# Attention rows: whole-array products issued as column tiles, and one transpose for two inputs

## The chip, the cores and the metric

The kernel runs on one core of one Trainium2 chip. The metric is device time in microseconds (us); lower is better. Before the change the median of three runs is 2716.82 us (2712.19 to 2721.92).

## What is computed

The input x has 256 rows of 256 positions with 128 channels. Layer 0 is an attention along each row, with a normalised x as query source and kv_x as key and value source; layer 1 is a spectral network on the result. The change touches layer 0 alone, which is, cut to what matters:

```python
def _L0_conv_ref(q_x, kv_x, bias1, bias2, wq, wk, wv, wg, bg, wo, bo):
    H = 4
    C_HIDDEN = 32
    q = split_heads(jnp.einsum('...qi,oi->...qo', q_x, wq)) / np.sqrt(C_HIDDEN)
    k = split_heads(jnp.einsum('...ki,oi->...ko', kv_x, wk))
    v = split_heads(jnp.einsum('...ki,oi->...ko', kv_x, wv))
    a = jnp.einsum('bshqd,bshkd->bshqk', q, k)
    a = a + bias1 + bias2
    a = jax.nn.softmax(a, axis=-1)
    o = jnp.einsum('bshqk,bshkd->bshqd', a, v)
    g = jax.nn.sigmoid(jnp.einsum('...qi,oi->...qo', q_x, wg) + bg)
    o = o * g
    return jnp.einsum('...qi,oi->...qo', o, wo) + bo

x = x + _L0_conv_ref(_gn(x), ...)
```

Everything is in 32-bit floats.

## The kernel before

`layer0` first reads x once for the statistics of the normalisation and folds them into wq and wg. Then the class `Rows` does the attention: its method `run` has a loop over i, the row, and rows are handled in pairs, g = i // 2. One pair of rows of x, and one of kv, is 512 positions by 128 channels. Layer 1 follows and isn't touched.

The order of instructions on each engine is the order of the program (`tc.manual_schedule` over PE, ACT, DVE, POOL and SP), so each queue can be read off the loop. The loop is a software pipeline: at row i it does the scores of row i, the projections of row i + 1, and the weighted sum of row i - 1. The parts are:

- `load` (L259) fetches a pair in pieces of 32 channels, two pairs ahead. `turn` (L283) brings it to channels on partitions with two DVE transposes of 32x32 blocks (L288), into buffers xT (four of them) and kvT (two).
- `project` (L292) makes q (L295) and k (L296) of a row: two products of the whole 128x128 array with 256 columns each. ACT copies them out (L300).
- `values` (L302) makes v of a pair with four products of 128 columns (L306) and the gate's input g with one of 512 (L312).
- `scores` (L319): eight products (L327), one for each head and half of the keys. A head has 32 channels, so each uses 32 rows of the array (shape 32*128), and four heads run side by side. ACT takes the exponential (L336).
- `weigh` (L345): DVE (L348) and POOL (L353) multiply by the exponential of bias1, POOL adds the two halves of the keys (L358).
- `attend` (L361): eight products with 32 output channels each (L368, shape 128*32, four side by side), and four with ones for the denominators (L373). DVE multiplies by the gate and divides (L379, L380, L381).
- `out` (L383): the output projection, one product of 512 columns (L386), the addition of x (L388), a transpose back (L390), and the store to x1d. `squares` (L401) and `spectrum` (L406) prepare layer 1: the latter reads the pair back and makes four products of 129 columns (L411).

PE's queue in an even row is L327, L295, L296, L386, L411, L368, L373; in an odd row L327, L295, L296, L306, L312, L368, L373. DVE's is L348, then L388 and L390 (even) or the two of L288 (odd), then L379, L380, L381. In PSUM, `ps_a` has four buffers, which the projections, v, g, wo, u and the weighted sum take in turn.

A PE shape is written as rows*columns of the array that an instruction uses: 128*128 is the whole array, 128*32 a column tile, 32*128 a row tile.

Of the kernel before, what the change touches and what calls it, by code (L numbers as in the profile page):

```python
# [10 lines left out]
FP = mybir.dt.float32  # L11
# [7 lines left out]
P = 128  # L19
# [177 lines left out]
class Rows:  # L197
# [72 lines left out]
    def run(self):  # L270
        tc, NS = self.tc, self.NS
        nc = tc.nc
        ctx, wT, rows, raw = self.ctx, self.wT, self.rows, self.raw
        b1T, b2T, bad = self.b1T, self.b2T, self.bad
        wk = ctx.enter_context(tc.tile_pool(name="l0wk", bufs=2))
        ps_s = ctx.enter_context(tc.tile_pool(name="l0s", bufs=1, space=PSUM))
        ps_a = ctx.enter_context(tc.tile_pool(name="l0a", bufs=4, space=PSUM))
        pairs = {}

        def row(s):  # L280
            return pairs[s // 2], slice(256 * (s % 2), 256 * (s % 2) + 256)

        def turn(g):  # L283
            t = raw.pop(g)
            p = pairs[g] = {}
            for k, (n, bufs) in enumerate((("xT", 4), ("kvT", 2))):
                p[n] = wk.tile([P, 512], FP, tag=n, name=f"{n}_{g}", bufs=bufs)
                nc.vector.transpose(p[n], t[:, k].rearrange("p b c -> p (b c)"))  # L288
            if g + 2 < NS // 2:
                self.load(g + 2)  # L290

        def project(s):  # L292
            p, q = row(s)
            ps = ps_a.tile([P, 512], FP, tag="a", name=f"qk_{s}")
            nc.tensor.matmul(ps[:, 0:256], self.wn["wq"], p["xT"][:, q], start=True, stop=True)  # L295
            nc.tensor.matmul(ps[:, 256:512], wT["wk"], p["kvT"][:, q], start=True, stop=True)  # L296
            r = rows[s] = {}
            r["qkT"] = wk.tile([P, 512], FP, tag="qkT", name=f"qkT_{s}")

            nc.scalar.activation(r["qkT"], ps, AF.Identity, bias=self.qb)  # L300

        def values(g):  # L302
            p = pairs[g]
            ps = ps_a.tile([P, 512], FP, tag="a", name=f"v_{g}")
            for c in range(4):
                nc.tensor.matmul(  # L306
                    ps[:, c * P : (c + 1) * P], p["kvT"][:, c * P : (c + 1) * P], wT["wv"], start=True, stop=True
                )
            p["v"] = wk.tile([P, 4, P], FP, tag="v", name=f"v_{g}")
            nc.scalar.copy(p["v"].rearrange("p c d -> p (c d)"), ps)  # L310
            p["g"] = ps_a.tile([P, 512], FP, tag="a", name=f"g_{g}")
            nc.tensor.matmul(p["g"], self.wn["wg"], p["xT"], start=True, stop=True)  # L312

        def gates(g):
            p = pairs[g]
# [67 lines left out]
        def out(g):  # L383
            p = pairs[g]
            ps = ps_a.tile([P, 512], FP, tag="a", name=f"wo_{g}")
            nc.tensor.matmul(ps, wT["wo"], p.pop("gate"), start=True, stop=True)  # L386
            xT = p["xT"]
            nc.vector.scalar_tensor_tensor(xT, ps, self.bo, xT, ALU.add, ALU.add)  # L388
            t = wk.tile([P, 16, 32], FP, tag="xb", name=f"x1b_{g}", bufs=1)
            nc.vector.transpose(t.rearrange("p b c -> p (b c)"), xT)  # L390
            pieces = self.x1d[2 * g : 2 * g + 2].rearrange("s (b t) c -> t (s b) c", t=32)
            for a in range(4):
                ch = slice(32 * a, 32 * a + 32)
                nc.sync.dma_start(pieces[:, :, ch], t[ch])
# [11 lines left out]
        def spectrum(g):  # L406
            x1 = pairs.pop(g)["x1"]
            ps = ps_a.tile([P, 512], FP, tag="a", name=f"u_{g}")
            for i in range(2):
                for j in range(2):  # L410
                    nc.tensor.matmul(  # L411
                        ps[:, 129 * i : 129 * i + 129], x1[:, i, j, :], self.adft[:, j, :],
                        start=(j == 0), stop=(j == 1),
                    )
            nc.scalar.copy(
                self.U[:, :, 2 * g : 2 * g + 2], ps[:, 0:258].rearrange("p (s f) -> p f s", s=2)
            )
# [3 lines left out]

        with tc.manual_schedule(engines={ENG.PE, ENG.Activation, ENG.DVE, ENG.Pool, ENG.SP}):
            turn(0)
            for i in range(-1, NS + 5):
                g, odd = i // 2, i % 2
# [7 lines left out]
                if i + 1 < NS:  # L433
                    project(i + 1)
# [5 lines left out]
                if odd and whole(g + 1):  # L440
                    values(g + 1)
                if odd and whole(g + 2):
                    turn(g + 2)
                if not odd and whole(g - 2):
                    out(g - 2)
                if not odd and whole(g - 3):
                    spectrum(g - 3)
                if 8 <= i < 16:
                    k, h = divmod(i - 8, 4)
# [131 lines left out]
def layer1(tc, I, C, ident, x1d, upool, U, Q2, groups, out):  # L581
# [9 lines left out]
    with ExitStack() as ctx:  # L591
# [908 lines left out]
        def first_modes(a, wp, mk, psum, gts):  # L1500
# [41 lines left out]
            for c in range(4):  # L1542
                synth_modes(wp, psum.pool, Z, P, h.Gd1, f"g1{a}", turned=True, chunk=c, ptag=psum.tag, gts=gts,
                            queues=(nc.gpsimd, nc.scalar))
                yield 2.4
                if c == 0:
                    yield next(tail)
                    yield next(tail)
                if c == 1:
                    run(tail)  # L1550
                    nc.vector.tensor_mul(h.bl0, h.bl0, h.row[:, 0:P])

                    ps = h.row
                    nc.tensor.matmul(ps[:, 256:257], blk[0], sig, start=True, stop=False)
                    nc.tensor.matmul(ps[:, 256:257], ident, ch[:, 2:3], start=False, stop=True)
                    nc.vector.tensor_copy(h.col[:, 13:14], ps[:, 256:257])
                    turned = mk("m", [P, 4, P], f"turned_{a}")
                    for j in range(4):
                        t = turned[:, j].rearrange("k (b d x) -> k b d x", b=2, d=2)
                        nc.vector.tensor_copy(  # L1560
                            t[:, :: (-1 if j & 2 else 1), :: (-1 if j & 1 else 1)],
                            ident.rearrange("k (b d x) -> k b d x", b=2, d=2),
                        )
                    for j in range(4):
                        nc.tensor.matmul(
                            ps[:, 260 + 2 * j : 262 + 2 * j], turned[:, j], h.col[:, 12:14],
                            start=True, stop=True,
                        )
                    nc.vector.tensor_copy(h.turn, ps[:, 260:268])
# [100 lines left out]
        def second_modes(a, wp, mk, psum, gts, yts):  # L1670
# [62 lines left out]
            for c in range(4):  # L1733
                if c == 2:
                    ps = psum.tile(f"cvps_{a}")
                    for i in range(4):
                        for r in range(2):
                            nc.tensor.matmul(
                                ps[:, 0:P], F[:, i, r, :], Z[:, i, r, :],
                                start=(i == 0 and r == 0), stop=(i == 3 and r == 1),  # L1740
                            )
                    cv = mk("m", [P, P], f"cv_{a}")
                    nc.vector.tensor_mul(cv, blk[1], ps[:, 0:P])
                synth_modes(wp, psum.pool, Z, P, h.Gd2, f"g2{a}", chunk=c, ptag=psum.tag, gts=gts,
                            queues=(nc.sync if a else nc.gpsimd, nc.scalar))
                yield 2.4
                if c == 0:
                    yield next(tail)
                    yield next(tail)
                if c == 1:  # L1750
                    run(tail)

                    for i in range(4):
                        r = slice(32 * i, 32 * i + 32)
                        v = h.row[r, 0:P].rearrange("k (b d x) -> k b d x", b=2, d=2)
                        nc.vector.tensor_tensor(
                            h.bl0[r].rearrange("k (b d x) -> k b d x", b=2, d=2),
                            v[:, :: (-1 if i & 2 else 1), :: (-1 if i & 1 else 1)],
                            bc(bc(blk[1][r, r], 1, 2), 1, 2), ALU.mult,
                        )  # L1760
# [362 lines left out]
```

## Time and profile before

| what | value |
|---|---|
| runs, median (lowest to highest) | 2716.82 us (2712.19 to 2721.92) |
| the profiled execution, and its span | 2722.32 us, 2720.5 us |
| instructions in the profile | 66879, of them 26560 products and 26560 weight loads on PE |
| PE busy | 2480.5 us (91%) |
| DVE busy | 2051.3 us (75%) |
| ACT busy | 1420.7 us (52%) |
| POOL busy | 1480.1 us (54%) |
| mean granted PE clock | 0.943 |
| row loop (first to last scores) | 114.6 to 1475.0 us |

The profile is one execution. PE is the matrix engine, PEld its weight loads, DVE, ACT and POOL the vector, scalar and general engines, SP the queue that issues transfers. The page cuts the span into 40 slices and gives a busy share in tenths for each. In a timeline line the columns are start, length, engine, source line, operation, output and inputs, and, for products, the shape and the elements of one instruction; xN says how many instructions are merged. In a line of a stretch the columns after the bounds are its length, then busy time and instruction count of PE, PEld, DVE, ACT and POOL, then granted clock, share of the transfer engines and GB/s. [...] consecutive products overlap and rates are read from start to start. One fp32 product of the source appears as two instructions.

### The profile page before, as it was taken

To read this page: it belongs to the slowest core of one execution; us is meant where nothing else is said; L and a number is where in the kernel's file an instruction comes from. 1 tells how busy PE (TensorE), PEld (TensorE's weight loads), DVE (VectorE), ACT (ScalarE), POOL (GpSimd) and SP (SyncE) were. 2 spreads that over 40 slices of the span, in tenths; PEclk is the share of its full clock that TensorE was granted. 3 is DMA by queue.
4 is the path that set the end of the run, shared out by engine and by line. 5 is a ranking of instruction groups with operands and counts; after the bars stand their busy time and mean duration, and the time that the engine had idled before them with its cause. 6 is when DMAs were issued, how large, how long until landed. Compare 5 with 4: busy or idle time off the path is not lost. (4 is left out here: it accounts for less than half of the span.)

```text
span 2720.5 us, 66879 instructions
## 1 busy us (share of the span) xinstructions
PE 2480.5 (91%) x26560; PEld 1648.3 (61%) x26560; DVE 2051.3 (75%) x3014; ACT 1420.7 (52%) x2718; POOL 1480.1 (54%) x1042
## 2 busy tenths in 40 slices
PE   7799999999999999999998899999988978898754
PEld 6566666666666666666665557787664566454522
DVE  7799999999999999999997438466645645455455
ACT  0277777778777787777776213100015501555232
POOL 0288999999998999999997003001135511111211
PEclk8899999999999999999999899999988987999755
DMA  9655555555555555555553010788987774997599
GB/s 369 192 98 98 101 99 101 101 100 99 102 100 100 100 98 101 100 98 103 99 101 71 20 57 1 250 273 266 316 290 237 258 240 129 333 358 258 185 378 345
DMA packets 1017841, 457.62 MB, mean 168 GB/s; under 512 B 831095, under 2 KB 947274, under 8 KB 1011129
## 3 DMA queue, kind: packets, MB, share of 16 engines
q1 hardware_dynamic: 977720, 363.13, 53.3%
q0 software_dynamic: 22912, 81.80, 7.8%
q10 hardware_dynamic: 16896, 8.39, 1.1%
q8 instruction: 212, 3.47, 0.5%
q14 instruction: 101, 0.82, 0.1%
HBM read 317.89 MB, written 135.27 MB: 167 GB/s over the span
## 5 line engine op out<-in xcount | busy, mean ns | idle before, releaser
L353 POOL TENSOR_TENSOR e<-e,b1T 128x1024 f32<-128x1024 f32 x256 | 606.1, 2367 | 203.8 <-ACT e L336 128.1
L358 POOL TENSOR_TENSOR es<-e 128x512 f32<-128x512 f32 x512 | 640.2, 1272 | 0.0
L380 DVE RECIPROCAL av<-av 128x256 f32<-128x256 f32 x256 | 452.1, 1766 | 8.8
L336 ACT ACTIVATE sc<-sc,b2T 128x512 f32<-128x512 f32 x512 | 338.8, 662 | 179.6 <-PE sc L327 171.3
L336 ACT ACTIVATE e<-sc,b2T 128x512 f32<-128x512 f32 x512 | 324.3, 692 | 0.0
L348 DVE TENSOR_TENSOR e<-sc,b1T 128x1024 f32<-128x1024 f32 x256 | 310.4, 1213 | 9.2 <-ACT sc L336 6.2
L327 PE MATMUL sc<-qkT 32*128 32x256 f32 x4096 | 293.6, 400 | 1.8 <-DVE e L348 1.8
L1381 PE MATMUL yps<-xt,mpT 128*128 128x256 f32 x1024 | 252.4, 398 | 27.1 <-DMA xt<-x1d 12.7
L368 PE MATMUL av<-e,v 128*32 128x256 f32 x4096 | 274.5, 385 | 2.2 <-DVE gate L381 1.9
L327 PEld LDWEIGHTS sc<-qkT 32*128 32x128 f32 x4096 | 185.3, 184 | 113.7 <-issue 100.9
L1381 PEld LDWEIGHTS yps<-xt,mpT 128*128 128x128 f32 x1024 | 195.8, 197 | 73.0 <-DVE yt L1393 17.0
L368 PEld LDWEIGHTS av<-e,v 128*32 128x32 f32 x4096 | 107.6, 109 | 159.3 <-PE v L306 94.0
L1397 POOL DMA_DIRECT2D yd<-yt x32 | 17.4, 545 | 320.7 <-DVE yt L1393 320.7
L295 PE MATMUL qk<-xT,wn_wq 128*128 128x256 f32 x512 | 179.4, 432 | 0.5 <-DVE hbg L230 0.5
L411 PEld LDWEIGHTS u<-adft,x 128*128 128x128 f32 x1024 | 135.7, 194 | 72.3 <-issue 62.9
L300 ACT ACTIVATE qkT<-qk,qb 128x512 f32<-128x512 f32 x256 | 174.0, 680 | 5.3 <-issue 5.3
L404 ACT ACTIVATE xT<-xT 128x256 f32<-128x256 f32 x256 | 104.4, 408 | 108.2 <-DVE x1b L390 106.3
L373 PE MATMUL av<-es,ones 128*32 128x256 f32 x2048 | 159.4, 379 | 1.4 <-POOL es L358 1.4
L1784 ACT ACTIVATE blocks<-h2ps,col 128x512 f32<-128x512 f32 x128 | 88.8, 778 | 128.5 <-PE h2ps L1248 128.5
L296 PE MATMUL qk<-kvT,wT_wk 128*128 128x256 f32 x512 | 152.7, 380 | 0.0
L379 DVE SCALAR_TENSOR_TENSOR gate<-gate,av 128x256 f32<-128x256 f32 x256 | 107.5, 420 | 53.5 <-PE av L373 40.1
L411 PE MATMUL u<-adft,x 128*128 128x129 f32 x1024 | 137.7, 278 | 8.5 <-DMA x<-x1d 8.4
(537 smaller groups left out, 4377.6 us busy)
## 6 DMA issues: line engine op xcount, KB each, us to landing
xt<-x1d SPq DMA_DIRECT2D x128, 512.0 KB, 6.7
xb<-in_x_dram SPq DMA_DIRECT2D x32, 1024.0 KB, 8.2
xk<-in_x_dram SPq DMA_DIRECT2D x512, 64.0 KB, 2.6
xk<-in_L_conv_kv_x_dram SPq DMA_DIRECT2D x512, 64.0 KB, 2.5
x1d<-x1b SPq DMA_DIRECT2D x512, 64.0 KB, 2.0
x<-x1d SPq DMA_DIRECT2D x128, 256.0 KB, 3.1
y<-yd SPq DMA_DIRECT2D x62, 512.0 KB, 7.0
gs<-Gd SPq DMA_DIRECT2D x384, 64.0 KB, 5.6
```

The lines of the kernel that those rows point to most:

```text
L295: nc.tensor.matmul(ps[:, 0:256], self.wn["wq"], p["xT"][:, q], start=True, stop=True)
L300: nc.scalar.activation(r["qkT"], ps, AF.Identity, bias=self.qb)
L327: nc.tensor.matmul(sc[h // 2][:, h % 2, c * 256 : (c + 1) * 256], qkT[p, 256 + c * P : 256 + (c + 1) * P], qkT[p, 0:256], start=True, stop ...
L336: nc.scalar.activation(r["e"][1][:, :, c, :] if hp else z, z, AF.Exp, bias=b2T[:, c, s : s + 1])
L348: nc.vector.tensor_tensor(r["e"][0].rearrange("p h c q -> p (h c q)"), r.pop("sc").rearrange("p h x -> p (h x)"), b1T[:, 0:2].rearrange("p ...
L353: nc.gpsimd.tensor_tensor(e1, e1, b1T[:, 2:4].rearrange("p h c q -> p (h c q)"), ALU.mult)
L358: nc.gpsimd.tensor_tensor(es, e[:, :, 0, :], e[:, :, 1, :], ALU.add)
L368: nc.tensor.matmul(ps[hd, 0:256], p["v"][:, 2 * (s % 2) + c, hd], r["e"][h // 2][:, h % 2, c, :], start=(c == 0), stop=(c == 1),)
L373: nc.tensor.matmul(ps[32 * h : 32 * h + 32, 256:512], self.ones, r["es"][h // 2][:, h % 2, :], start=True, stop=True,)
L380: nc.vector.reciprocal(rd, rd)
L411: nc.tensor.matmul(ps[:, 129 * i : 129 * i + 129], x1[:, i, j, :], self.adft[:, j, :], start=(j == 0), stop=(j == 1),)
L1381: nc.tensor.matmul(rows_of(ps[j]), mpT[:, sc, tt], by_turn(xt[:, sc])[:, j], start=(sc == 0), stop=False,)
```

## The change

All products of the row loop that used the whole array (q, k, v, g, wo, u) are issued as four products of 32 output channels or positions each, by the new helper `by_columns`: the same moving operand, a quarter of the stationary one, and the output to its quarter of the partitions. The two transposes of `turn` become one instruction, which writes x's and kv's part to two slots of a single buffer `turned` with six slots: four that rotate for x, two for kv. The rest of the loop, the order included, stays.

```diff
+        turned = wk.tile([P, 6, 512], FP, name="turned", bufs=1)
+
+        def by_columns(out, w, src, start=True, stop=True):
+            for h in range(4):
+                hd = slice(32 * h, 32 * h + 32)
+                nc.tensor.matmul(out[hd], w[:, hd], src, start=start, stop=stop)
...
         def turn(g):
             t = raw.pop(g)
-            p = pairs[g] = {}
-            for k, (n, bufs) in enumerate((("xT", 4), ("kvT", 2))):
-                p[n] = wk.tile([P, 512], FP, tag=n, name=f"{n}_{g}", bufs=bufs)
-                nc.vector.transpose(p[n], t[:, k].rearrange("p b c -> p (b c)"))
+            a, b = g % 4, 4 + g % 2
+            nc.vector.transpose(
+                turned[:, a : b + 1 : b - a].rearrange("p k (b c) -> p k b c", c=32), t
+            )
+            pairs[g] = {"xT": turned[:, a], "kvT": turned[:, b]}
...
-            nc.tensor.matmul(ps[:, 0:256], self.wn["wq"], p["xT"][:, q], start=True, stop=True)
-            nc.tensor.matmul(ps[:, 256:512], wT["wk"], p["kvT"][:, q], start=True, stop=True)
+            by_columns(ps[:, 0:256], self.wn["wq"], p["xT"][:, q])
+            by_columns(ps[:, 256:512], wT["wk"], p["kvT"][:, q])
...
             for c in range(4):
-                nc.tensor.matmul(
-                    ps[:, c * P : (c + 1) * P], p["kvT"][:, c * P : (c + 1) * P], wT["wv"], start=True, stop=True
-                )
+                by_columns(ps[:, c * P : (c + 1) * P], p["kvT"][:, c * P : (c + 1) * P], wT["wv"])
...
-            nc.tensor.matmul(p["g"], self.wn["wg"], p["xT"], start=True, stop=True)
+            by_columns(p["g"], self.wn["wg"], p["xT"])
...
-            nc.tensor.matmul(ps, wT["wo"], p.pop("gate"), start=True, stop=True)
+            by_columns(ps, wT["wo"], p.pop("gate"))
...
-                    nc.tensor.matmul(
-                        ps[:, 129 * i : 129 * i + 129], x1[:, i, j, :], self.adft[:, j, :],
-                        start=(j == 0), stop=(j == 1),
+                    by_columns(
+                        ps[:, 129 * i : 129 * i + 129], x1[:, i, j, :], self.adft[:, j, :], j == 0, j == 1
                     )
```

## The prediction

> **What bounds the kernel now.** I read the page's engine totals and its 40 slices first, to find the stage that the change touches and which engine fills it.
>
> ```profile
> PE   7799999999999999999998899999988978898754
> DVE  7799999999999999999997438466645645455455
> PEclk8899999999999999999999899999988987999755
> ```
>
> The row loop lies in slices 3 to 22 (its first product starts at 109 us, its last near 1498). PE and DVE both show nines there, at full clock. To tell which of the two is the limit, I asked for the busy time in a stretch of ten pairs of rows.
>
> ```profile
> 700.00:806.40 106.40, 106.40 (x1085) 68.60 (x1081) 100.62 (x121) 84.22 (x171) 96.48 (x60) 1.00 0.57 100
> ```
>
> PE is busy for all of the 106.40 us, DVE for 100.62, ACT 84.22, POOL 96.48. So a pair of rows takes 10.64 us, PE sets it, and DVE would need 10.06. The timeline of DVE agrees: in both rows it reaches L379 and has to wait for PE's L373.
>
> ```profile
> 709.25 1.21 DVE L348 TENSOR_TENSOR e<-sc,b1T 128x1024 f32<-128x1024 f32 x1
> 710.38 0.70 DVE L288 STREAM_TRANSPOSE xT<-xk 128x512 f32<-128x512 f32 x1
> 711.01 0.67 DVE L288 STREAM_TRANSPOSE kvT<-xk 128x512 f32<-128x512 f32 x1
> 711.97 0.42 DVE L379 SCALAR_TENSOR_TENSOR gate<-gate,av 128x256 f32<-128x256 f32 x1 [0.30 <-PE av L373]
> ```
>
> "Busy" on PE isn't work at its peak, so I took PE's own timeline of one pair and subtracted start from start.
>
> ```profile
> 704.07 1.06 PE L411 MATMUL u<-adft,x 128*128 128x129 f32 x8
> 705.06 1.07 PE L368 MATMUL av<-e,v 128*32 128x256 f32 x16
> 705.94 0.61 PE L373 MATMUL av<-es,ones 128*32 128x256 f32 x8
> 706.49 1.15 PE L327 MATMUL sc<-qkT 32*128 32x256 f32 x16
> 707.57 0.70 PE L295 MATMUL qk<-xT,wn_wq 128*128 128x256 f32 x2
> 708.10 0.59 PE L296 MATMUL qk<-kvT,wT_wk 128*128 128x256 f32 x2
> 708.53 1.05 PE L306 MATMUL v<-wT_wv,kvT 128*128 128x128 f32 x8
> 709.42 1.02 PE L312 MATMUL g<-xT,wn_wg 128*128 128x512 f32 x2
> 710.38 0.85 PE L368 MATMUL av<-e,v 128*32 128x256 f32 x12
> ```
>
> Each product in the source is two instructions here (two passes). L296 to L306 is 708.53 - 708.10 = 0.43 us with nothing in between: two passes of 256 columns, 0.215 each. That is the streaming rate, 0.43 us for each 256 columns of a whole-array product. L368 to L373 is 0.88 us for 16 instructions, which are four passes of four column tiles side by side: 0.22 a pass. So four 128x32 tiles together go as fast as one 128x128 product; tiling neither gains nor loses streaming time. What exceeds streaming sits at the changes of shape (128*128, 128*32, 32*128 in the rows):
> - 128*32 to 32*128 (L373 to L327): 0.55 - 0.43 = 0.12 before the first product, and L327's first weights 0.10 (1.08 from L327 to L295 = 0.86 streaming + 0.10 + 0.11 of the next change). 0.22 together.
> - 32*128 to 128*128: that 0.11, and L295's first weights, 0.53 - 0.43 = 0.10. 0.21 together.
> - 128*128 to 128*32: L312 to L368 is 0.96 for 0.86 of streaming, 0.10, and L368's first weights 0.88 - 0.86 = 0.02. 0.12 together.
>
> A row pays 0.22 + 0.21 + 0.12 = 0.55 us, a pair 1.10. Check: a pair streams 5636 columns (scores 1024, L368 and L373 1536, q and k 1024, v, g and wo 512 each, u 516) at 0.43/256, which is 9.47; 9.47 + 1.10 = 10.57 of 10.64.
>
> [...] 0.10 to 0.12 us at each change of shape, and none from L368 to L373, which changes tiles only. [...] The trace shows 0.10 exposed for L327 and L295 and 0.02 for L368. [...] in the trace 512 elements take 711.01 - 710.38 = 0.63 from start to start.
>
> **The change part by part.**
> *PE shapes.* q, k, v, g, wo and u become 128*32. Order and count of columns stay. Per row one change goes altogether (128*128 to 128*32, 0.12 us). [...] its first weights are 32 columns: 0.13 in place of 0.21, 0.08 saved. The change into L327 stays at 0.22. Saved: 0.20 us a row, 256 rows: 51 us. All of it is on PE, which is the bound, so it comes out of the time as long as PE remains the bound.
> *More PE instructions.* Per pair, q and k 8 instructions become 32, v 8 to 32, u 8 to 32, g and wo 2 to 8 each: 84 products more and as many weight loads. 216 PE instructions in 10.64 us become 384, or 38 per us. Tightest in v and u: 4 products and 4 loads for each 128 columns. Layer 1 of the same trace has exactly v's form (128*32, 128 columns), and a denser one:
>
> ```profile
> 2200.79 1.95 PE L1695 MATMUL f1ps<-YT,k_efwd 128*32 128x128 f32 x64
> ```
>
> ```profile
> 2313.81:2315.81 2.00, 2.00 (x132) 1.83 (x140) 0.06 (x1) 0.17 (x1) 1.49 (x2) 1.00 0.53 151
> ```
>
> 64 products are 16 passes; 1.95 less the tail of one product (0.27) is 1.68 over 15 passes plus the first load, 0.11 a pass, which is streaming rate. The second line has 132 products and 140 loads in 2 us, 136 instructions per us. So issue costs nothing in bursts. That 38 per us hold over 1.3 ms is less certain: layer 1 has 32 per us over 40 us (646 and 646 in 2300 to 2340). I take 0.
> *Four tiles on one moving operand.* L368, L373 and L1695 give each tile its own; here all four stream the same addresses. L644 (g11gp, 32*64) has two tiles on one moving operand and is the row of 136 per us, so at least two don't disturb each other. I take 0. Bounds: [...] a stretch f of the 3076 columns affected (5.17 us a pair) costs 661 us times f.
> *The merged transpose.* Two of 0.63 and 0.62 start to start become one of 1024 elements. The nearest row of that size is L348: 710.38 - 709.25 = 1.13. I take 1.15, 0.10 saved a pair. It is worth nothing: with PE at 10.64 - 0.40 = 10.24, DVE at 10.06 - 0.10 still waits. Both sides: free up to about 1.25 + 0.18 = 1.43 us; above that each 0.1 costs 13 us, and at 1.25 + 0.58 = 1.83 the gain is gone. Its wait covers the x and the kv pieces at once; both were loaded two pairs earlier and land in 2.6 us.
> *One buffer for all pairs.* Slots repeat after four (x) and two (kv) pairs as the separate buffers did. The instruction order on DVE shows the transpose waiting for its loads alone, and the products for what they waited for before. Cost 0.
> *What is late next.* A row falls to 5.12 us. POOL's 9.65 a pair (4.82 a row) fits. Waits into PE have room: L327 at 706.49 needs ACT's exp (L336, ended near 705.5) and L348 (705.1), 1.0 us; L368 at 705.06 needs DVE's previous L381 (704.0), 1.0 us; L373 needs POOL's sums of the row before (705.1), 0.8 us. Each loop of dependence turns with the same row time, so 0.2 us less leaves them short of binding. Next is DVE, 0.3 us a pair away.
>
> **The sum.** Profiled execution 2722.3 us (span 2720.5): less 51, 2671. The median of the three runs, 2716.8, is 5.5 lower, and I forecast from it: 2716.8 - 51 = 2666, rounded to 2667 for the first and last rows, which lack some of the changes.
>
> **Rivals.**
> 1. Half the gain. The entry from 32*128 into 128*32 occurs nowhere in the row loop before; if it costs 0.21 like the entry into 128*128, only 0.12 a row goes: 31 us, 2686. DVE or POOL binding in some rows would look the same. For it: that one transition is unseen, and DVE is close. Against: both its parts are seen singly.
> 2. No change: the stalls belong to waits on other instructions and not to the shapes, or DVE takes over because the merged transpose comes near 1.8 us. 2717. Against: the stall has one size at every change of shape, and from L368 to L373, which also waits on another engine, there is none.
> 3. Slower: the four tiles that stream one operand get in each other's way, in the six products that now do so. It decides from f = 51/661 = 7.7% on. At 15%, so that a pass of 256 columns takes 0.25 instead of 0.215, it costs 99 less 51: 2765. For it: no row shows four tiles on one operand, and the instruction stream nearly doubles for 1.3 ms. Against: L1695, L368 and L644 at the full rate.
>
> **How the numbers follow.** Forecast 0.65, half gain 0.17, no change 0.05, slower 0.13. The likeliest holds 2656 to 2676 (u and v may shed their 0.03 us above streaming as well, 8 us). The range goes on to the half gain: 2655 to 2692. A difference under 0.3% could not be told from none. Faster by more: 0.65 + 0.17 = 0.82; within: 0.05; slower by more: 0.13.
>
> **What would show it.** Right: L368 follows the last product of u or g without the 0.10; the start-to-start from the scores to q falls little, from q to k to 0.45; a pair takes 10.2 us; DVE's wait before its first multiplication shrinks to some 0.2 us and PE is still busy all the time. Wrong: q to k well over 0.45 (stretch), v above 0.9 (issue), a transpose above 1.4 us, or PE with gaps ahead of L368.

## The result, and the profile after

Over 14 runs of each kernel the changed one takes 2712.22 us (median; 2706.84 to 2729.14) against 2717.85 us before (2709.14 to 2725.27). The ratio is 0.9991, with an interval of 0.9974 to 1.0009: no difference that can be told, where 2667 us had been forecast. The profiled execution has a span of 2705.0 us.

First the slices of the page after. The row loop still fills slices 3 to 22, though PE's share over the loop, by the busy time between 114.6 and 1475 us, fell from 1354.50 to 1317.52 us.

```profile
PE   6699999999999999999998899998989978898754
DVE  7799999999989999999998437566645645465355
PEclk9899999999999999999999899999999988999865
```

The same stretch of 106.4 us as before, by engines (length, then busy time and count for PE, PEld, DVE, ACT, POOL):

```profile
700.00:806.40 106.40, 101.28 (x1856) 60.02 (x1848) 96.23 (x108) 81.39 (x165) 95.38 (x59) 0.98 0.57 100
```

PE was busy for all of it before, and now has 5 us of gaps. So something other than PE decides part of the time. Still, PE's timeline of a pair shows what was forecast of the shapes:

```profile
703.57 1.07 PE L285 MATMUL u<-adft,x 128*32 128x129 f32 x32
704.45 1.04 PE L374 MATMUL av<-e,v 128*32 128x256 f32 x16
705.31 0.61 PE L379 MATMUL av<-es,ones 128*32 128x256 f32 x8
705.86 1.15 PE L333 MATMUL sc<-qkT 32*128 32x256 f32 x16
706.93 0.64 PE L285 MATMUL qk<-turned,wn_wq 128*32 128x256 f32 x8
707.39 0.61 PE L285 MATMUL qk<-turned,wT_wk 128*32 128x256 f32 x8
707.82 1.06 PE L285 MATMUL v<-wT_wv,turned 128*32 128x128 f32 x32
708.69 1.04 PE L285 MATMUL g<-turned,wn_wg 128*32 128x512 f32 x8
709.55 1.05 PE L374 MATMUL av<-e,v 128*32 128x256 f32 x16
```

From u to the weighted sum it is now 0.88 us from start to start (0.99 before), from g to it 0.86 (0.96), from q to k 0.46 (0.53), and v takes 0.87 (0.89). All six products, with four tiles on one operand, stream at the rate of before: 0.215 us for 256 columns in each of the two passes of a product. From scores to scores this row takes 5.10 us (5.32 before). The merged transpose (L293) takes 1233 ns on average.

The next pair looks different. PE's timeline again, 9 us on:

```profile
712.92 1.04 PE L285 MATMUL wo<-gate,wT_wo 128*32 128x512 f32 x8
714.66 1.09 PE L285 MATMUL u<-adft,x 128*32 128x129 f32 x32 [0.69 <-DMA x<-x1d]
```

wo streams for 0.86 us, so u could start at 713.78. It starts at 714.66, because its operand x, the pair's result read back from x1d, hasn't landed. The list of waits of the row loop (who waits for whom: total us, times, longest) has this line before the change and after:

```profile
PE u L411 <- DMA x<-x1d: 8.4, 6, 5.5
```

```profile
PE u L285 <- DMA x<-x1d: 42.3, 49, 4.5
```

Both sides of the account come from the starts of the scores. 255 rows at 5.321 - 5.103 us gain 55.6 us. Against 5.103 a row, 56.7 us of delay lie in the loop after the change (62 rows are more than 0.3 us late); against 5.321 it was 2.8 before. The loop, first to last scores, went from 1359.6 to 1357.9 us. Where nothing delays u it starts 0.86 us after wo; beyond that its starts are late by 54.3 us in all after the change and by 5.1 before (the list of waits has less, since it counts only the idle time of PE). So the whole gain was made, and nearly all of it was given back in u.

Why is the landing late now? SP's queue shows the round trip: store to x1d (four pieces), wait for their landing, read back, then the next loads. Before:

```profile
701.06 1.94 SPq L267 DMA_DIRECT2D xk<-in_x_dram  x4
703.05 2.09 SPq L267 DMA_DIRECT2D xk<-in_L_conv_kv_x_dram  x4
706.57 1.96 SPq L394 DMA_DIRECT2D x1d<-x1b  x4
710.06 0.40 SPq L399 DMA_DIRECT2D x<-x1d  x1
```

After:

```profile
700.79 3.02 SPq L267 DMA_DIRECT2D xk<-in_x_dram  x4
703.85 2.09 SPq L267 DMA_DIRECT2D xk<-in_L_conv_kv_x_dram  x4
706.15 1.96 SPq L400 DMA_DIRECT2D x1d<-x1b  x4
711.36 0.40 SPq L405 DMA_DIRECT2D x<-x1d  x1
```

From the first store to the read it was 3.5 us there and is 5.2 here. Over 105 pairs (pair 10 to 114, by the starts of these two instructions) the median went from 3.60 to 4.50 us and the mean from 3.80 to 4.46. The read itself is as before (median 3.1 us to landing before, 3.0 after). Before, u was due 8.14 us after the first store, so the read could be issued up to 5.1 us after it. With a pair 0.43 us shorter, 4.7 are left. Three of the 105 pairs were later than 4.67 us before, 41 after. The waits come mostly every second pair, and the mean pair is back at 10.66 us.

### The profile page after: what moved, and what is told of

It reads as the page before. It is cut to its first block, busy times and chain, and to the rows that moved or that the text cites. A ratio compares the mean times of both kernels' runs of the same rounds, so it can differ in the third digit from the quotient of the medians.

```text
span 2705.0 us, 88255 instructions
## 1 busy us (share of the span) xinstructions
PE 2424.3 (90%) x37312; PEld 1547.0 (57%) x37312; DVE 2034.9 (75%) x2886; ACT 1424.4 (53%) x2718; POOL 1486.7 (55%) x1042
## 3 DMA queue, kind: packets, MB, share of 16 engines
q8 instruction: 296, 4.85, 0.8%
## 5 line engine op out<-in xcount | busy, mean ns | idle before, releaser
L1386 PE MATMUL yps<-xt,mpT 128*128 128x256 f32 x1024 | 246.2, 391 | 27.2 <-DVE yt L1398 13.8
L1386 PEld LDWEIGHTS yps<-xt,mpT 128*128 128x128 f32 x1024 | 191.9, 193 | 70.7 <-DVE yt L1398 19.1
L374 PEld LDWEIGHTS av<-e,v 128*32 128x32 f32 x4096 | 136.4, 110 | 120.1 <-issue 37.8
L285 PEld LDWEIGHTS u<-adft,x 128*32 128x32 f32 x4096 | 114.6, 111 | 141.5 <-ACT qkT L308 66.4
L285 PE MATMUL u<-adft,x 128*32 128x129 f32 x4096 | 140.0, 277 | 46.7 <-DMA x<-x1d 42.3
L285 PE MATMUL qk<-turned,wn_wq 128*32 128x256 f32 x2048 | 164.1, 392 | 1.8 <-DVE turned L293 1.8
L293 DVE STREAM_TRANSPOSE turned<-xk 128x1024 f32<-128x1024 f32 x128 | 157.8, 1233 | 0.1
L285 PE MATMUL qk<-turned,wT_wk 128*32 128x256 f32 x2048 | 157.8, 380 | 0.0
```

Source lines behind the costliest of these rows:

```text
L285: nc.tensor.matmul(out[hd], w[:, hd], src, start=start, stop=stop)
L293: nc.vector.transpose(turned[:, a : b + 1 : b - a].rearrange("p k (b c) -> p k b c", c=32), t)
L374: nc.tensor.matmul(ps[hd, 0:256], p["v"][:, 2 * (s % 2) + c, hd], r["e"][h // 2][:, h % 2, c, :], start=(c == 0), stop=(c == 1),)
L1386: nc.tensor.matmul(rows_of(ps[j]), mpT[:, sc, tt], by_turn(xt[:, sc])[:, j], start=(sc == 0), stop=False,)
```

## The experiments

Theory A: the round trip through x1d has no room left once a pair takes 10.2 us. Theory B: the loss is due to the doubled stream of PE instructions or a loaded SP queue, and u only shows it. Theory C: the merged transpose shifts the loads. Each kernel was compared with the kernel before on the same chip; ratios have 95% intervals.

### u one pair later

```diff
-            p["x1"] = wk.tile([P, 2, 2, P], FP, tag="x1", name=f"x1_{g}", bufs=1)
+            p["x1"] = wk.tile([P, 2, 2, P], FP, tag="x1", name=f"x1_{g}", bufs=2)
...
-            for i in range(-1, NS + 5):
+            for i in range(-1, NS + 7):
...
-                if not odd and whole(g - 3):
-                    spectrum(g - 3)
+                if not odd and whole(g - 4):
+                    spectrum(g - 4)
```

> The changed kernel, with u of a pair (spectrum) one pair of rows later and two buffers for x1, so that the read-back of x1d has one pair's time more. Theory A (the round trip of a pair through x1d - store, wait for its landing, read, landing - has no slack left once a pair takes 10.2 us, and PE waits for it in u): the waits of u for x1d go (42 us before), a pair takes 10.2 us throughout and the time is 2660 to 2672 us. Theory B (the time is lost to the doubled stream of PE instructions or to a loaded SP queue, and the wait in u only shows it): the wait moves to another product, the time stays at 2705 to 2718 us. Theory C (the merged transpose shifts the loads, which then delay the stores): part of the gain, 2680 to 2700.

Measured: 2673.61 us, ratio 0.9842 (0.9819 to 0.9864), 2 us above what theory A had given. The line of waits and the stretch at 700 us in this kernel:

```profile
PE u L285 <- DMA x<-x1d: 6.0, 2, 3.4
```

```profile
700.00:806.40 106.40, 106.40 (x2008) 63.69 (x2000) 103.08 (x116) 87.72 (x177) 101.13 (x63) 1.00 0.60 104
```

PE has no gaps again in this stretch, and DVE (103.08 of 106.40) and POOL (101.13) are close behind. The row loop takes 1307.7 us, 51.9 less than before. That the whole execution gains 42 us in the medians and not 52 is within what the rest of the program varies: outside the loop the profiles of this study took between 1347 and 1369 us, with the same code. B in the form that the time is lost whatever u does falls: the instructions are all still there. C falls with the next two runs.

### The same on the kernel before, and each half of the change alone

The second kernel is the kernel before with the same later u; the third has the column tiles with the two old transposes; the fourth has the merged transpose with the products over the whole array. The part that makes the third from the changed kernel:

```diff
+            p = pairs[g] = {}
+            for k, (n, bufs) in enumerate((("xT", 4), ("kvT", 2))):
+                p[n] = wk.tile([P, 512], FP, tag=n, name=f"{n}_{g}", bufs=bufs)
+                nc.vector.transpose(p[n], t[:, k].rearrange("p b c -> p (b c)"))
-            nc.vector.transpose(
-                turned[:, a : b + 1 : b - a].rearrange("p k (b c) -> p k b c", c=32), t
-            )
```

> The kernel before with the same later u and nothing else. Control: it has 8 us of waits for x1d in all, most of them at the start. All theories: 2710 to 2718 us, no difference that can be told. If it is faster by more than 10 us, moving u pays by itself and e1 says less about A.

> Column tiles alone, with the two transposes and their own buffers as before. Theory A: as the change, 2706 to 2718 us, with the same waits of u for x1d. Theory B: the same. Theory C (the merged transpose is what delays the loads and the stores): 2665 to 2690 us, few waits in u.

> The merged transpose and the common buffer alone, all products over the whole array as before. All theories: PE sets the time, so 2712 to 2720 us, DVE's wait for PE 0.1 us a pair longer. Theory C: up to 10 us slower, with waits of u for x1d.

Measured: 2714.03 us (ratio 0.9998, 0.9981 to 1.0014), 2713.39 us (0.9992, 0.9977 to 1.0007) and 2717.34 us (0.9996, 0.9983 to 1.0009). Without the column tiles a later u gives nothing. Column tiles alone do what the change does: rows of 5.10 us where u doesn't wait, and 41.2 us of waits of u for x1d. The merged transpose does nothing here.

### The transposes apart, once PE is faster

> The kernel of e1 with the two transposes apart again. DVE then needs 10.06 us a pair against PE's 10.21. Theory A: as e1, 2665 to 2680 us, and DVE's wait for PE is the smaller by 0.1 us a pair. If the merged transpose matters once PE is faster (DVE nearly the bound), it is 5 to 15 us slower than e1.

Measured: 2665.88 us, ratio 0.9811 (0.9786 to 0.9835), which overlaps that of the later u with the merged transpose. So the merge isn't needed for the gain either. These two kernels beat both the kernel before and the changed one, and can't be told from each other. The profiled execution of this one was the slowest of its six (2686.97 us), and its list of waits shows another wait for the same stores: x1b, from which they are made, has one buffer, and DVE's next transpose back waited until it was free, 19.1 us in 24 places.

### Which products have to be tiles

With the later u kept, q and k were put back on the whole array in one kernel; in another q and k alone were tiles.

```diff
-            by_columns(ps[:, 0:256], self.wn["wq"], p["xT"][:, q])
-            by_columns(ps[:, 256:512], wT["wk"], p["kvT"][:, q])
+            nc.tensor.matmul(ps[:, 0:256], self.wn["wq"], p["xT"][:, q], start=True, stop=True)
+            nc.tensor.matmul(ps[:, 256:512], wT["wk"], p["kvT"][:, q], start=True, stop=True)
```

> The kernel of e1 with q and k over the whole array again, the other products as column tiles. By the prices of the shape changes (0.22 into the scores, 0.21 out of them into the whole array, 0.12 from there into column tiles) a row has all three again, 0.55 us as before the change: 2710 to 2718 us, a pair 10.6 us. If column tiles are faster by themselves (not by the changes of shape), most of the gain stays: 2680 to 2695.

> The kernel of e1 with q and k alone as column tiles, and v, g, wo and u over the whole array. A row has four changes of shape: into the scores 0.22, out into column tiles 0.13, into the whole array 0.21, into column tiles 0.12, together 0.68 in place of 0.35 in e1: 0.33 us a row more than e1, 84 us: 2750 to 2765 us, slower than the kernel before by 34 us. If the gain were in proportion to the products that are tiled, it would lie between e1 and the kernel before.

Measured: 2719.55 us (1.0007, 0.9991 to 1.0023) and 2748.21 us (1.0118, 1.009 to 1.0146), each 2 us outside what was expected. It is the number of changes of shape that counts, not how many products are tiled: with v, g, wo and u as tiles and q and k whole, three changes a row and no gain; with q and k as tiles alone, four changes and 32.6 us slower, for 34 forecast. PE's timeline of the latter shows where the fourth change lies:

```profile
705.67 0.64 PE L285 MATMUL qk<-turned,wn_wq 128*32 128x256 f32 x8
706.12 0.61 PE L285 MATMUL qk<-turned,wT_wk 128*32 128x256 f32 x8
706.67 1.12 PE L394 MATMUL wo<-gate,wT_wo 128*128 128x512 f32 x2
707.63 1.06 PE L419 MATMUL u<-adft,x 128*128 128x129 f32 x8
```

k streams for 0.43 us, and wo follows after 0.55; wo streams for 0.86 and u follows after 0.96. That is 0.12 in front of wo and 0.10 in front of u, as much as q took longer than its streaming in the kernel before: 0.22 for one change into the whole array, for 0.21 expected.

### A deadline moved by 1.3 us and by 0.9 us

If the landing is late by 0.1 to 1.3 us, moving u back in PE's queue by that much should do, with one buffer. First behind the whole of `attend`:

```diff
-                if not odd and whole(g - 3):
-                    spectrum(g - 3)
...
                 if 0 <= i - 1 < NS:
                     attend(i - 1)
+                if not odd and whole(g - 3):
+                    spectrum(g - 3)
```

> The changed kernel with u (spectrum) moved behind the weighted sum of the same row (attend), so that its product comes 1.3 us later in PE's queue; one x1 buffer, nothing else. Theory A (the read-back of x1d comes late for u by 0.1 to 1.3 us): most of the 42 us of waits go, 2670 to 2690 us, with a rest where a landing is later than 1.3 us. If it is not a matter of a deadline but of load on the queues, the waits stay near 40 us and the time at 2705 to 2718 us.

Measured: 2732.9 us, ratio 1.0059 (1.0038 to 1.0081), slower, against the expectation. No wait of u for x1d is left in the loop; but the products with the ones come earlier now, and meet POOL, which hasn't made their sums:

```profile
PEld av L379 <- POOL es L364: 57.8, 128, 1.1
```

One wait per pair, 0.45 us each. The prediction had put the room of this wait at 0.8 us, and u, now behind these products, had stood for 0.88 us in front of them. The deadline was cured and another made. So u was put between the two halves of `attend`, where the products with the ones keep their place:

```diff
-        def attend(s):
+        def attend(s, between=None):
...
+            if between is not None:
+                spectrum(between)
             for h in range(4):
                 nc.tensor.matmul(
                     ps[32 * h : 32 * h + 32, 256:512], self.ones, r["es"][h // 2][:, h % 2, :],
...
-                if not odd and whole(g - 3):
-                    spectrum(g - 3)
...
+                u = g - 3 if not odd and whole(g - 3) else None
                 if 0 <= i - 1 < NS:
-                    attend(i - 1)
+                    attend(i - 1, u)
...
```

> The changed kernel with u between the products of the weighted sum and those with the ones in PE's queue: u comes 0.87 us later than in the changed kernel, and the products with the ones stay where they were, so they don't meet POOL's sums early as in e5. One x1 buffer. Theory A: the waits of u for x1d, of which most are under 0.9 us, fall from 42 us to 15 or less, no wait for POOL: 2672 to 2695 us. If a deadline isn't the matter: 2705 us or more with u's waits unchanged.

Its line in the list of waits of the row loop:

```profile
PE u L285 <- DMA x<-x1d: 15.7, 14, 5.0
```

Measured: 2687.46 us, ratio 0.9898 (0.9875 to 0.9921), with 15.7 us of waits in place of 42.3 (15 or less had been expected). With 0.9 us more room for u, more than half of the gain is there; with a pair's time, nearly all of it. That is theory A, in doses.

### SP relieved of the wait

The read-back is issued from ACT's queue, so that SP needn't hold the next loads behind the landing of the stores.

```diff
-            nc.sync.dma_start(p["x1"], self.x1d[2 * g : 2 * g + 2].rearrange("s (j p) c -> p s j c", p=P))
+            nc.scalar.dma_start(p["x1"], self.x1d[2 * g : 2 * g + 2].rearrange("s (j p) c -> p s j c", p=P))
...
                 if odd and whole(g - 2):
-                    again(g - 2)
                     squares(g - 2)
...
+                if odd and whole(g - 2):
+                    again(g - 2)
                 if odd and whole(g + 2):
                     turn(g + 2)
```

> The changed kernel with the read-back of x1d issued from ACT's queue behind the copy of v, u where the change has it. SP then no longer holds the next loads behind the wait for the stores' landing. Theory A1 (the stores land late because SP is kept so busy by that wait that loads and stores come back to back): store to read falls from 4.5 us towards 3.6, u's waits fall by half or more, 2670 to 2695 us. Theory A2 (the deadline is simply too near at 10.2 us a pair, and the read itself starts no earlier): the waits stay, 2700 to 2720 us; ACT's own wait in front of the read can make it slower still.

Measured: 2728.64 us, ratio 1.0048 (1.0035 to 1.0061), 36.5 us of waits of u, and 4.53 us from store to read (median). The read again follows the landing of the stores by 0.1 us, so ACT doesn't hold it back. That is theory A2, at a time above its 2720: it isn't SP's wait that makes the landing late.

### What makes the landing late

Among the kernels so far the time from store to read goes with the number of PE instructions rather than with the time of a pair. It is 3.60 us (median) with 20 PE instructions per us and a mean pair of 10.66 us (before), 3.85 with 32 and 10.61 (q and k whole), 4.50 with 36 and 10.66 (the change). The profile shows transfers of instructions as well. Their queue has, before and after (packets, MB, share of 16 engines):

```profile
q8 instruction: 212, 3.47, 0.5%
```

```profile
q8 instruction: 296, 4.85, 0.8%
```

Each packet of this queue is 16 KB (3.47 MB in 212) and takes 1.1 us on average (1.12 before, 1.13 after). In the 105 pairs there are 0.87 of them a pair before and 1.52 after. Sorting the pairs by whether such a fetch overlaps the stretch from store to read gives a median of 3.58 us without and 4.04 with one before the change, 3.62 without (18 pairs) and 4.60 with one (87 pairs) after. Of SP's 1260 issues of loads and stores in these pairs, 122 took over 0.7 us after the change, and a fetch overlapped 108 of them; before, 43, and 41 of them.

That is a correlation, so instructions were added to the kernel before, without more columns or changes of shape:

```diff
-            for c in range(2):
-                for h in range(4):
+            for n in range(2):
+                for c in range(2):
+                    for h in range(4):
...
-                        ps[hd, 0:256], p["v"][:, 2 * (s % 2) + c, hd], r["e"][h // 2][:, h % 2, c, :],
+                            ps[hd, q2], p["v"][:, 2 * (s % 2) + c, hd], r["e"][h // 2][:, h % 2, c, q2],
...
+            for n in range(4):
+                for h in range(4):
+                    nc.tensor.matmul(
+                        ps[32 * h : 32 * h + 32, 256 + 64 * n : 320 + 64 * n], self.ones,
+                        r["es"][h // 2][:, h % 2, 64 * n : 64 * n + 64], start=True, stop=True,
+                    )
```

> The kernel before, with the weighted sum's products issued in halves of 128 columns and those with the ones in quarters of 64: same shapes, same order, same columns, but 160 PE instructions more a pair (376 in place of 216, the changed kernel has 384). Theory F (the added instructions have to be fetched, in packets of 16 KB and 1.1 us on the transfer engines, and a fetch between a pair's store and its read delays the landing): fetches a pair go from 0.87 to about 1.5 and the median from store to read from 3.6 to 4.3 us or more, at an unchanged 10.6 to 10.8 us a pair; u has 1.5 us of room here, so few waits, and the time is that of e12 within 10 us. Theory G (the landing is late because a pair is shorter or because column tiles read more): store to read stays at 3.6 us.

> The same with u one pair later: no deadline, so it shows what the smaller products cost on PE by themselves, against e2. Up to 2% slower than the kernel before (2715 to 2770 us); store to read as in e11.

Measured: 2734.56 us (1.0057, 1.0032 to 1.0082) and 2725.27 us (1.0035, 1.0023 to 1.0048). Fetches went to 1.50 a pair. Store to read rose to a median of 3.95 us (mean 4.11) in the first and 3.94 (4.07) in the second, at pairs of 10.74 and 10.69 us. So more instructions alone lengthen this trip from the first store to the read, as theory F says, but to less than the 4.3 us expected: they bring 0.3 of the 0.66 us that the mean rose in the change, and pairs later than 4.67 us go from 3 to 21 of 105, not to 41. At an unshortened pair u has room for that: it waits 4.4 us for x1d in the first of the two. In the second, PE's own rows are slightly longer (5.346 us, 5.321 before), so the smaller products aren't quite free.

The rest isn't a matter of shorter pairs: with u behind `attend` a pair takes 10.79 us, and the trip still has a median of 4.52 us, with 1.52 fetches a pair. The kept traces point to the moment at which the fetch starts. Over the same 105 pairs of each of the fourteen kernels:

| start of the fetch, from the first store | mean trip, us | pairs |
|---|---|---|
| no fetch in the 3.6 us from the first store | 3.66 | 472 |
| over 0.75 us before it | 3.73 | 110 |
| up to 0.75 us before it | 4.10 | 222 |
| 0 to 0.5 us after it | 4.51 | 185 |
| 0.5 to 1 us after it | 4.64 | 143 |
| 1 to 1.5 us after it | 4.85 | 97 |
| 1.5 to 2 us after it | 5.04 | 78 |
| 2 to 2.5 us after it | 5.18 | 56 |
| 2.5 to 3 us after it | 5.35 | 53 |
| 3 to 3.6 us after it | 4.27 | 54 |

A fetch that starts 1 to 3 us after the first store is met by none of the 105 pairs before, by 12 in the kernel with added instructions, and by 31 in the changed one. A table made from the other thirteen kernels gives these three mean trips of 3.84, 4.17 and 4.42 us, where 3.80, 4.11 and 4.46 were measured. At the same moment of the fetch, the five kernels without the new column tiles and the five with them and one buffer for x1 differ by 0.2 us at most. So most of the remainder goes with when the fetches fall, and little is left for the reads of the column tiles or for the length of a pair. This is read from the traces and not shown by an experiment: no kernel moved the fetches alone, and why they fall later in the changed kernel stays open.

It also bears on the waits in every second pair. With u one pair later nothing waits for the trips, and they alternate all the same: of its 49 trips over 4.67 us only 9 follow another such trip. So that a late pair gives the next read more time can't be the only reason. In the changed kernel, with 1.52 fetches a pair, one starts 1.8 to 2.6 us after the first store in each of the pairs 45, 47, 49, 51 and 53, whose trips take 4.83 to 5.21 us, and none starts from 0 to 4.5 us after it in the four pairs between, with 3.58 to 4.12 us.

## Why the prediction was wrong

- PE bounds the row loop, and pays for changes of shape: right. It was forecast at 0.20 us a row and measured at 0.218 (5.321 to 5.103). Of the forecast, 0.08 came from q's first weights with 32 columns, an estimate of 0.02 us, as at L368, in place of 0.10; 0.03 was measured (q to k 0.46 for 0.43 of streaming). The loop with u one pair later gained 51.9 us, for 51 forecast. That these two are so near is in part luck: the rows gained 55.6 us, and 6.5 us of other delays lay in that loop against 2.8 in the loop before. The runs with three and four changes a row came out within 2 us of the ranges that the prices gave.
- DVE has room: right in the sum. But it was read as waiting for L373 in both rows of a pair, and the trace has 0.30 us in the row of the transposes and only 0.11 us, too little to be listed as a wait, in the other.
- Four tiles on one moving operand: 0, and 0 was measured. The slower rival, which rested on a stretch there, falls with q to k at 0.46 us.
- The merged transpose: 1.23 us against the 1.15 taken, below the 1.43 from which it would count. Worth nothing, as forecast.
- One buffer for all pairs: no wait came of it.
- **The step that failed is "What is late next".** It went through the waits of L327, L368 and L373 and found 0.8 to 1.0 us of room in each. It left out the one product that waits for a transfer, u (L411): its operand goes from DVE through SP, a store, a landing, a read and another landing. There was room here too, 8.14 us for 3.6 + 3.1, some 1.4 us. But the claim that "each loop of dependence turns with the same row time" isn't true of this one: its parts are transfers, and when the rows got shorter the read stayed near 3.0 us and the part before it went from 3.60 to 4.50.
- **Behind it, "More PE instructions" was put at 0** because PE issues them fast enough, which it does here: 37.7 a us (2008 products and 2000 loads in 106.40 us) without a gap in the kernel with u one pair later. Their fetch, 296 packets in place of 212, wasn't counted. In the medians the longer trip took 0.90 of those 1.4 us and the shorter pair 0.43; the 0.1 us left doesn't cover the longer half of the trips. More instructions at the old pair cost u hardly any wait; a shorter pair without more instructions wasn't run.
- The rival "no change" had a chance of 0.05 for other reasons (waits that the shapes don't explain, a transpose near 1.8 us); neither is what happened. The right rival would have been a round trip of transfers that doesn't get shorter with the rows and becomes the bound of the loop; the list of waits before had it with 8.4 us in six places, all but 0.6 us outside 300 to 1400 us.

## What to carry to other kernels

Before counting on a gain in a loop, list every wait in it for a transfer, and above all round trips through memory, with the room each has; here the shorter pair took 0.43 us of 1.4 us of room, and more instructions alone lengthened the median trip from 3.60 to 3.95 us. If an operand makes such a trip, give it a whole turn of the loop more in the same change (here 2 KB per partition for a second buffer, and the waits of u fell from 42.3 to 6.0 us). Moving the waiting instruction only a little back in its queue helped too (0.9 us brought the waits to 15.7 us), but what moves ahead of it meets its own producers earlier: 1.3 us brought 57.8 us of waits for POOL's sums.

## What the runs showed that was not expected

- Instructions were fetched in packets of 16 KB that took 1.1 us each on average. With none between a pair's first store and its read the trip took 3.6 to 3.7 us in the median in each of the fourteen kernels; with one, 4.0 to 5.0, the more the later after the first store the fetch starts, up to 3 us.
- Four 128*32 tiles that stream the same operand ran at the rate of one 128*128 product, 0.215 us for a pass of 256 columns of fp32 (two passes a product), with v at 64 products and loads in 0.87 us.
- A change of shape cost 0.10 to 0.12 us before the next product starts, and the first product behind it then took longer: q by 0.10 us where its weights have 128 columns and by 0.03 where they have 32, the weighted sum (32) by 0.02.
